# First q stacks computed in place, four first products moved into block 0, v's bias sent through the projection

## The chip, the core and the metric

The kernel runs on one NeuronCore of a Trainium2 chip. The metric is the device time of one execution in microseconds (us); a time is the median of several runs. The engines are TensorE (PE; PEld is its weight load), VectorE (DVE), ScalarE (ACT), GpSimd (POOL) and SyncE (SP, which only issues DMAs). Each works through its own instruction list in order and waits on semaphores. TensorE writes to PSUM; ACT and DVE read PSUM and write SBUF.

## What is computed

Layer 0 is attention over the 4096 pixels of each of 4 images with 128 channels, layer 1 two quantized 3x3 convolutions with batch norm. Only layer 0 bears on the change:

```python
x_norm = group_norm(x, norm_w, norm_b)                  # 8 groups
qkv = einsum('oc,bchw->bohw', qkv_w, x_norm) + qkv_b
q, k, v = split(qkv)                                    # 4 heads of 32 channels
attn = softmax(einsum('bhid,bhjd->bhij', q, k) * d**-0.5)
out = einsum('bhij,bhjd->bhid', attn, v)
out = einsum('oc,bchw->bohw', proj_w, out) + proj_b
x = x + out
```

Each row of the softmax sums to one, so a constant added to v comes out of the attention unchanged, and the projection of that constant can be added to proj_b.

## The kernel before

The kernel tries `_fast_body` and has a general version behind it that isn't run with these inputs. Everything named here is in `_fast_body`, which writes the order of all instructions by hand.

**Tiling.** The 4096 pixels of an image are NB = 8 chunks of 512 (FB) for k, v and q, and NK = 32 key tiles of 128. A block is one image and one chunk of 512 queries: 32 blocks. For each key tile of a block, `scores` (L442) makes two score halves of 128 keys by 2 heads by 512 queries with 4 matmuls each, and ACT turns each into exponentials p (L444). `weights` (L456) multiplies v by p in two halves of 4 matmuls each and adds into acc. Most p tiles are added into r by DVE (L469, L471); those of the key tiles in MOVED are added into rm by DMAs from POOL (L464, L466). At a block's end, `finish_parts` copies acc, merges rm into r, takes the sums l, inverts, weighs, projects (po), adds the bias bp and the residual (L547) and stores y0.

**Groups.** The main loop is `run_scores(3); run_weights(3)`: a group is three score halves, then three weight halves. TensorE runs three score halves ahead. `schedule` attaches side work to weight halves of a block: `at_half(p, f)` calls f after half p. `ends[i]` is the last half of the block's group i. `visit(i, first, second, evacuate, split=False)` puts both halves of a product after `ends[i]` and its emptying one half later. That is in the next group, so on ACT it stands behind the three exponentials of that group.

**Products.** A k, q or v product is one chunk through the normed weights `wn`: `banded` (L317) makes it with one matmul for each head into a band of 32 partitions. k and q are split into a high and a low part in fp32r: ACT writes the high part with the bias (L351), DVE the low part (L352). Both parts are staged, written to DRAM (kd, qd; L356) and loaded back as stacks, in which each head has its high and its low part on two bands of 32 partitions (`load_k` L411, `load_q` L422). v is emptied by DVE alone, which adds v's bias (L371).

**Buffers.** [...]The pool `pss` has three tiles of two banks, named "s", for scores; the pool `psa` has two tiles of one bank, named "a". In a block acc holds one of these two; everything else that TensorE writes outside scores (products, sums, projection, the small matmuls of the norm) goes through the other. During the start-up k and q products use `pss`. In a block the parts of k are staged in one buffer named "k", those of q1 in one named "q"; in the start-up they use tiles of the pool of p.

**Start-up.** Eight chunks of image 0 are loaded into two tiles. DVE takes their statistics (L597). `norm_parts` works out the norm in small steps: `four` makes wn and a vector c (scaled mean less bias), `five` and `six` the biases of k and q from c (L281, L282, L286), `five_v` and `six_v` v's bias as a 128 by 128 tile, the same on all partitions (L291, L296). Then the list

```python
for what, j in (("k", 0), ("q", 0), ("k", 1), ("v", 0), ("k", 2), ("v", 1), ("k", 3), ("v", 2),
                ("k", 4), ("v", 3)):
```

is worked off, and the scores begin. The stacks of k0 and q0 don't go through DRAM: `direct` copies them by eight DMAs each from the staged parts (L402 for k from SP and POOL, L404 for q from ACT, SP and POOL). The other eight first products (k5, v4, k6, v5, k7, q1, v6, v7) are attached to block 0, after the ends 0, 2, 4 and so on to 14 in steps of two groups. q2 to q7 of image 0 are made in block 1.

**Later images.** The norm of image b + 1 is prepared during image b. In the fourth block of image 0 (third of images 1 and 2), `five` is called after `ends[1]`, `six` and `five_v` one half later, `six_v` two halves later, and the first k product of the next image follows after `ends[3]`.

Of the kernel before, what the change touches and what calls it, by code (L numbers as in the profile page):

```python
# [16 lines left out]
F32 = mybir.dt.float32  # L17
AF = mybir.ActivationFunctionType
ALU = mybir.AluOpType
# [3 lines left out]
P = 128  # L23
GROUP = 16
HEADS = 4
D = 32
TAPS = 9
FB = 512
# [50 lines left out]
def _fast_body(ctx, tc, x, norm_w, norm_b, qkv_wt, qkv_b, proj_wt, proj_b,  # L79
               w1, alpha1, gamma1, beta1, w2, alpha2, gamma2, beta2, out, cnt):  # L80
    nc = tc.nc
# [6 lines left out]
    KB = FB // P  # L88
# [26 lines left out]
    nw, nb = column(norm_w, "nw"), column(norm_b, "nb")  # L115
    wqkv = const.tile([P, 3 * P], F32, name="wqkv")
    nc.gpsimd.dma_start(out=wqkv, in_=qkv_wt)
    bkq = const.tile([P, 2], F32, name="bkq")
    nc.gpsimd.dma_start(out=bkq[:, 0:1], in_=qkv_b[P : 2 * P].rearrange("(c o) -> c o", o=1))
    nc.gpsimd.dma_start(out=bkq[:, 1:2], in_=qkv_b[0:P].rearrange("(c o) -> c o", o=1))  # L120
    bv = const.tile([P, P], F32, name="bv")
    nc.gpsimd.dma_start(out=bv, in_=qkv_b[2 * P : 3 * P].partition_broadcast(P))
    wp = const.tile([P, P], F32, name="wp")
    nc.gpsimd.dma_start(out=wp, in_=proj_wt)
    bp = column(proj_b, "bp")
# [101 lines left out]
    def f32(t):  # L227
        return t.bitcast(F32)
# [8 lines left out]

    norm = {}  # L240

    def norm_parts(b, st):
        mv = small.tile([P, 2], F32, name=f"mv{b}", tag="mv")
        mean = small.tile([P, 1], F32, name=f"mean{b}", tag="mean")
        dv = small.tile([P, 1], F32, name=f"dv{b}", tag="dv")
        gm = {}

        def zero():
            nc.vector.bn_aggr(mv, st.rearrange("p j s -> p (j s)"))


        def one():
# [12 lines left out]
        def four():  # L265
            r = rsqrt_eps(gm[1][:, 0:1], f"gr{b}")
            a = small.tile([P, 1], F32, name=f"ga{b}", tag="ga")
            nc.vector.tensor_tensor(a, r, nw, ALU.mult)
            c = small.tile([P, 1], F32, name=f"gc{b}", tag="gc")
            nc.vector.scalar_tensor_tensor(c, mean, a, nb, ALU.mult, ALU.subtract)  # L270
            wn = wpool.tile([P, 3 * P], F32, name=f"wn{b}", tag="wn")
            nc.vector.tensor_scalar(wn, wqkv, a, None, ALU.mult)
            cb = wpool.tile([P, P], F32, name=f"cb{b}", tag="cb")
            nc.vector.tensor_copy(cb, c.to_broadcast([P, P]))
            norm[b] = [wn, c, cb]


        def five():
            wn, c, cb = norm[b]
            gm[2] = psa.tile([P, FB], F32, name=f"gb{b}", tag="a")  # L280
            nc.tensor.matmul(gm[2][:, 0:1], wqkv[:, P : 2 * P], c, start=True, stop=True)  # L281
            nc.tensor.matmul(gm[2][:, 1:2], wqkv[:, 0:P], c, start=True, stop=True)  # L282

        def six():
            b2 = wpool.tile([P, 2], F32, name=f"b2_{b}", tag="b2")
            nc.vector.tensor_tensor(b2, bkq, gm[2][:, 0:2], ALU.subtract)  # L286
            norm[b][1] = b2

        def five_v():
            gm[3] = psa.tile([P, FB], F32, name=f"gw{b}", tag="a")  # L290
            nc.tensor.matmul(gm[3][:, 0:P], norm[b][2], wqkv[:, 2 * P : 3 * P],  # L291
                             start=True, stop=True)

        def six_v():
            bvn = wpool.tile([P, P], F32, name=f"bvn{b}", tag="bvn")
            nc.vector.tensor_tensor(bvn, bv, gm[3][:, 0:P], ALU.subtract)  # L296
            norm[b][2] = bvn

        return zero, one, two, three, four, five, six, five_v, six_v

# [18 lines left out]
    def project_parts(b, j, xin, start=False):  # L319
# [3 lines left out]
        ps = {}  # L323
# [23 lines left out]
        def parts(what, o, dst):  # L347
            t = staged(2, what)
            bias = norm[b][1][:, o : o + 1]
            hi, lo = (t[:, i, :].bitcast(F32R) for i in range(2))  # L350
            nc.scalar.activation(hi, ps[what], AF.Identity, bias=bias)  # L351
            nc.vector.scalar_tensor_tensor(lo, ps[what], bias, t[:, 0, :], ALU.add, ALU.subtract)  # L352
            if start and j == 0:
                direct(what, t)
            else:
                (nc.sync if start else nc.gpsimd).dma_start(out=dst[b, j].rearrange("s p n -> p s n"), in_=t)  # L356

# [7 lines left out]
        def evac_v():  # L365
            if b == 0:
                v = vs[b, j] = vpool.tile([P, KB, P], F32, name=f"v{b}_{j}", tag="v")
                v = v.rearrange("p i f -> p (i f)")
            else:
                v = staged(1, "v")[:, 0, :]  # L370
            nc.vector.tensor_tensor(v.rearrange("p (i f) -> p i f", f=P),  # L371
                                    ps["v"].rearrange("p (i f) -> p i f", f=P),
                                    norm[b][2].unsqueeze(1).to_broadcast([P, KB, P]), ALU.add)
            if b > 0:
                nc.gpsimd.dma_start(out=vd[b, j], in_=v)

# [6 lines left out]
    def k_tile(b, j):  # L383
        ks[b, j] = stack_tile(f"k{b}_{j}")[:, : 2 * FB].rearrange("p (g n) -> p g n", n=FB)
        return ks[b, j]

    def q_tile(b, j):
        qs[b, j] = qpool.tile([P, 2, 2, FB], F32R, name=f"q{b}_{j}", tag="q")
        return qs[b, j]

    def direct(what, t):

        u = k_tile(0, 0) if what == "k" else q_tile(0, 0)
        engines = (nc.sync, nc.gpsimd) if what == "k" else (nc.scalar, nc.sync, nc.gpsimd)
        for g in range(2):
            for c, s in enumerate((0, 2, 1, 3)):
                i, part = divmod(s, 2)
                h = 2 * g + i
                src = t[h * D : (h + 1) * D, :, :]
                eng = engines[(4 * g + c) % len(engines)]  # L400
                if what == "k":
                    eng.dma_start(out=f32(u)[s * D : (s + 1) * D, g, :], in_=src[:, part, :])  # L402
                else:
                    eng.dma_start(out=f32(u)[s * D : (s + 1) * D, g, :, :], in_=src)  # L404

    def load_k(b, j):
        k = k_tile(b, j)
        for s in range(4):
            i, part = divmod(s, 2)
            src = kd[b, j][part].rearrange("(g i d) n -> i d g n", i=2, d=D)  # L410
            nc.sync.dma_start(out=f32(k)[s * D : (s + 1) * D, :, :], in_=src[i])  # L411
# [61 lines left out]
    def finish_parts(n):  # L473
# [70 lines left out]
            banded(t["o"], wp, av)  # L544

        def store():
            nc.vector.scalar_tensor_tensor(t["x"], t["o"], bp, t["x"], ALU.add, ALU.add)  # L547
            nc.gpsimd.dma_start(out=y0[b][:, qb * FB : (qb + 1) * FB], in_=t["x"])

        return dict(copy=copy, merge=merge, sums=sums, sums_at_once=sums_at_once, bounds=bounds,  # L550
# [44 lines left out]
    st = small.tile([P, NB, 6], F32, name="st0", tag="st")  # L595
    for j in range(NB):
        nc.vector.bn_stats(st[:, j, :], halves[j // 4][:, j % 4, :])  # L597
    zero, one, two, three, four, five, six, five_v, six_v = norm_parts(0, st)
    zero()
    one()  # L600
    keep_warm(3)
# [11 lines left out]
        load_k(b, j)  # L613
        load_v(b, j)

    for what, j in (("k", 0), ("q", 0), ("k", 1), ("v", 0), ("k", 2), ("v", 1), ("k", 3), ("v", 2),
                    ("k", 4), ("v", 3)):
        for f in first_chunk(j, what, True):
            f()
        if what == "q":  # L620
            five_v()
            six_v()
        if what == "v":
            load_k(0, j + 1)

# [7 lines left out]
    def schedule(n, before):  # L633
# [5 lines left out]
        def at_half(p, f):  # L639
            todo.append((p, f))  # L640
# [25 lines left out]
        if n + 1 < len(blocks):  # L666
            add(22 if n == 0 else 14, lambda: load_q(*blocks[n + 1]))
        if n == 0:
            for i, what, j in ((0, "k", 5), (2, "v", 4), (4, "k", 6), (6, "v", 5), (8, "k", 7),
                               (10, "q", 1), (12, "v", 6), (14, "v", 7)):  # L670
                visit(i, *first_chunk(j, what, False), split=False)
                if what == "k":
                    at_half(ends[i] + 5, lambda j=j: load_k(0, j))
# [9 lines left out]
        if b + 1 < B:  # L683
# [10 lines left out]
            if qn == 2:  # L694
                at_half(ends[1], late[b][5])
                at_half(ends[1] + 1, late[b][6])
                at_half(ends[1] + 1, late[b][7])
                at_half(ends[1] + 2, late[b][8])
            if b == 0:
                chunks = {2: (), 3: (0, 1), 4: (2, 3), 5: (4, 5), 6: (6,), 7: (7,)}  # L700
            else:
                chunks = {1: (), 2: (0, 1), 3: (2, 3), 4: (4,), 5: (5,), 6: (6,), 7: (7,)}
# [708 lines left out]
```

## Time and profile before

| | |
|---|---|
| time, median of 3 runs | 2549.02 us (2548.26 to 2549.62) |
| the profiled execution | 2548.74 us, span 2547.0 us |
| granted TensorE clock, mean | 0.995 |
| first scores start | 26.66 us |
| weights of block 0 start | 31.91 us |
| TensorE busy in 34.2 to 92.0 us | 57.80 of 57.80 us |
| the same for ACT, DVE | 50.10, 49.16 us |
| low part (L352) of a k or q chunk | 0.75 us |
| high part (L351) | 0.69 us |
| v with its bias (L371) | 0.68 us |
| one addition to r (L471) | 2.29 us |

The profile is that of one execution; its times start with the span. Timeline rows give start and duration in us, the engine, the line, the operation, output and inputs with their shapes, and a count where neighbouring instructions of one kind are merged. Brackets hold how long the engine stood idle ahead of the row and what released it. In the chain of work that ended last, a piece lasts until the next begins. An fp32 matmul appears as two passes, so a count of 16 is 8 matmuls; the fp32r matmuls of the scores appear as one.

### The profile page before, as it was taken

The page shows a single profiled execution, that of the slowest core. Times are in us where ns is not written, and L with a number is a line of the kernel's source. Part 1 is how long each engine was busy: PE and PEld are TensorE (multiplying, and loading weights), DVE is VectorE, ACT ScalarE, POOL GpSimd, SP SyncE. Part 2 cuts the span into 40 slices and gives each one's busy share as a digit, 9 for nine tenths or more (in the row PEclk, how much of TensorE's full clock was granted, in tenths as well). Part 3 has the DMA queues.
Part 4 walks back from the last instruction along what each step waited for, and adds up shares of the span by engine and source line. Part 5 has one row for each costly group of instructions (what it writes and reads, how often), then busy time and mean ns, then how long its engine had stood idle before and what let it go on. Part 6 is the DMA issues. An engine that isn't in the chain of part 4 may idle for free.

```text
span 2547.0 us, 65043 instructions
## 1 busy us (share of the span) xinstructions
PE 2509.0 (99%) x28708; PEld 1503.6 (59%) x28708; DVE 2137.2 (84%) x1402; ACT 2087.4 (82%) x2278; POOL 281.6 (11%) x461
## 2 busy tenths in 40 slices
PE   9999999999999999999999999999999999999995
PEld 6555555555555555555555555555555555577774
DVE  6899888889988889889988888889999999954445
ACT  5999888999988999999988899989999999911224
POOL 2111111111011111110111111111000011000000
PEclk9999999999999999999999999999999999999998
DMA  6877667788757667797766666796666666745004
GB/s 193 192 185 169 168 173 181 171 203 182 184 132 190 170 152 169 164 231 164 173 163 172 157 166 158 191 203 150 149 138 144 146 145 149 150 90 160 1 1 166
DMA packets 148954, 403.86 MB, mean 159 GB/s; under 512 B 59416, under 2 KB 60184, under 8 KB 120120
## 3 DMA queue, kind: packets, MB, share of 16 engines
q0 software_dynamic: 45840, 280.39, 48.2%
q1 hardware_dynamic: 100952, 113.60, 16.9%
q10 hardware_dynamic: 1872, 5.64, 0.6%
q8 instruction: 227, 3.72, 0.6%
q14 instruction: 63, 0.52, 0.1%
HBM read 107.48 MB, written 56.42 MB: 64 GB/s over the span
## 4 chain that ended last, share of the span: by engine, by line
PE 92%; issue 3%; DMA 2%; DVE 1%; ACT 1%; ACTq 0%; POOL 0%; SPq 0%; POOLq 0%; DVEq 0%
PE s L442 41%; PE acc L456 36%; PE c L782 9%; DMA rm<-p 2%; PE l L488 1%; PE pq L317 1%; PE pk L317 1%; PE po L317 1%; PE pv L317 1%; DVE r L471 1%; ACT p L444 0%; ACT res L949 0%; DMA xh<-in_x_dram 0%; PE c_last L782 0%; DVE res L948 0%
## 5 line engine op out<-in xcount | busy, mean ns | idle before, releaser
L444 ACT ACTIVATE p<-s 128x1024 f32<-128x1024 f32 x2048 | 1950.5, 1032 | 201.6 <-PE s L442 154.5
L471 DVE TENSOR_TENSOR r<-r,p 128x2048 f32<-128x2048 f32 x768 | 1758.2, 2289 | 65.0 <-ACT p L444 14.5
L442 PE MATMUL s<-q,k 64*128 64x512 f32 x8192 | 1138.6, 409 | 1.7 <-ACT p L444 0.9
L456 PE MATMUL acc<-p,v 128*32 128x256 f32 x16384 | 1026.4, 383 | 0.0
L442 PEld LDWEIGHTS s<-q,k 64*128 64x128 f32 x8192 | 715.4, 184 | 410.3 <-issue 165.3
L456 PEld LDWEIGHTS acc<-p,v 128*32 128x32 f32 x16384 | 462.4, 109 | 483.7 <-issue 248.5
L466 POOL DMA_DIRECT2D rm<-p x160 | 139.5, 872 | 800.4 <-ACT p L444 535.5
L849 ACT COPY cv<-c 128x512 f32<-128x512 f32 x60 | 35.2, 586 | 200.1 <-DVE st L848 200.1
L782 PE MATMUL c<-hi,wq 128*128 128x512 f32 x540 | 139.1, 401 | 1.3 <-issue 1.3
L782 PE MATMUL c<-lo,wq 128*128 128x512 f32 x540 | 138.5, 400 | 0.0
L848 DVE BATCH_NORM_STATS2 st<-c 128x6 f32<-128x512 f32 x60 | 41.9, 699 | 103.9 <-PE c L782 83.4
L782 PEld LDWEIGHTS c<-hi,wq 128*128 128x128 f32 x540 | 101.2, 188 | 30.3 <-issue 2.1
L782 PEld LDWEIGHTS c<-lo,wq 128*128 128x128 f32 x540 | 101.6, 188 | 27.2
L352 DVE SCALAR_TENSOR_TENSOR kst<-pk,b,kst 128x512 fp32r<-128x512 f32 x32 | 24.0, 751 | 83.6 <-PE s L442 68.5
L469 DVE TENSOR_TENSOR r<-p,p 128x2048 f32<-128x2048 f32 x32 | 73.2, 2288 | 12.1 <-ACT p L444 11.1
L352 DVE SCALAR_TENSOR_TENSOR qst<-pq,b,qst 128x512 fp32r<-128x512 f32 x32 | 24.0, 751 | 58.2 <-PE s L442 47.3
L356 POOL DMA_DIRECT2D qd<-qst x31 | 23.6, 760 | 262.7 <-DVE qst L352 220.8
L492 POOL DMA_DIRECT2D r<-rm x31 | 26.2, 844 | 220.4 <-DMA rm<-p 95.1
L356 POOL DMA_DIRECT2D kd<-kst x27 | 20.0, 740 | 175.8 <-DVE kst L352 167.2
L488 PE MATMUL l<-r,ones 128*32 128x256 f32 (+1 forms) x504 | 37.7, 382 | 0.0
L464 POOL DMA_DIRECT2D rm<-p x32 | 17.8, 557 | 176.8 <-ACT p L444 93.4
L351 ACT ACTIVATE kst<-pk,b 128x512 fp32r<-128x512 f32 x32 | 22.3, 699 | 18.2 <-PE pk L317 18.2
(149 smaller groups left out, 739.3 us busy)
## 6 DMA issues: line engine op xcount, KB each, us to landing
rm<-p POOLq DMA_DIRECT2D x192, 1024.0 KB, 7.9
q<-qd SPq DMA_DIRECT2D x248, 128.0 KB
r<-rm POOLq DMA_DIRECT2D x31, 1024.0 KB, 7.6
x<-in_x_dram SPq DMA_DIRECT2D x86, 256.0 KB
k<-kd SPq DMA_DIRECT2D x124, 128.0 KB
qd<-qst POOLq DMA_DIRECT2D x31, 512.0 KB, 5.3
kd<-kst POOLq DMA_DIRECT2D x27, 512.0 KB, 4.8
y<-x POOLq DMA_DIRECT2D x32, 256.0 KB, 6.2
```

The lines of the kernel that those rows point to most:

```text
L317: nc.tensor.matmul(out[cs, :], w[:, cs], x, start=True, stop=True)
L352: nc.vector.scalar_tensor_tensor(lo, ps[what], bias, t[:, 0, :], ALU.add, ALU.subtract)
L356: (nc.sync if start else nc.gpsimd).dma_start(out=dst[b, j].rearrange("s p n -> p s n"), in_=t)
L442: nc.tensor.matmul(s[:, i, :], k[r, half, c0 : c0 + P], q[r, half, part, :], start=(part == 0), stop=(part == 1))
L444: nc.scalar.activation(pts[step][:, 2 * half : 2 * half + 2, :], s, AF.Exp, scale=SCALE)
L456: nc.tensor.matmul(acc[n][h * D : (h + 1) * D, cs], v[:, kt % KB, h * D : (h + 1) * D], pt[:, h, cs], start=(kt == 0 and half == 0), stop= ...
L466: nc.gpsimd.dma_start(out=msum[n], in_=pt, accum_op=ALU.add)
L469: nc.vector.tensor_tensor(rsum[n], pts[step - 1], pt, ALU.add)
L471: nc.vector.tensor_tensor(rsum[n], rsum[n], pt, ALU.add)
L488: nc.tensor.matmul(t["l"][h * D : (h + 1) * D, cs], ones, r[:, h, cs], start=first, stop=end)
L782: nc.tensor.matmul(ps.rearrange("p (r w) -> p r w", w=W), w[:, tap, :], part[:, r0 + kh : r0 + kh + RB, kw : kw + W], start=(n == 0), stop ...
L848: nc.vector.bn_stats(st[:, b * NB + c, :], ps[:, j, :])
```

## The change

- q0 is computed straight into its stack (`direct_q`). For each pair of heads g, four matmuls of 512 columns with the 32 weight columns of a head go into four bands, so that each head's product stands on two bands. ACT writes the high part and DVE the low part of all 128 partitions into the q tile, with biases that are laid out in the same way: four more small DMAs load them into columns 2 and 3 of bkq, and `five` makes eight more one-column matmuls for image 0. Nothing is staged, and `direct` is left with k0.
- The start-up list loses k3, v2, k4 and v3; they are attached to block 0, in which twelve products now follow the ends 0, 1, 2, 4, 5, 6, 8, 9, 10, 11, 13 and 14.
- v is copied without its bias. The bias is a column u; `seven_v` multiplies it by the projection's weights and `eight_v` adds the result to bp. The output takes this column in place of bp. In the start-up both are called behind the list; for later images `seven_v` is attached to `ends[3]`, `eight_v` to the half after it.

```diff
-    bkq = const.tile([P, 2], F32, name="bkq")
+    bkq = const.tile([P, 4], F32, name="bkq")
...
-    bv = const.tile([P, P], F32, name="bv")
-    nc.gpsimd.dma_start(out=bv, in_=qkv_b[2 * P : 3 * P].partition_broadcast(P))
+    for band in range(4):
+        nc.gpsimd.dma_start(
+            out=bkq[band * D : (band + 1) * D, 2:4],
+            in_=qkv_b[0:P].rearrange("(g i d) -> i d g", i=2, d=D)[band // 2])
+    bv = const.tile([P, 1], F32, name="bv")
+    nc.gpsimd.dma_start(out=bv, in_=qkv_b[2 * P : 3 * P].rearrange("(c o) -> c o", o=1))
...
-            cb = wpool.tile([P, P], F32, name=f"cb{b}", tag="cb")
-            nc.vector.tensor_copy(cb, c.to_broadcast([P, P]))
...
+            if b == 0:
+                for g in range(2):
+                    for band in range(4):
+                        h = 2 * g + band // 2
+                        nc.tensor.matmul(gm[2][band * D : (band + 1) * D, 2 + g : 3 + g],
+                                         wqkv[:, h * D : (h + 1) * D], c, start=True, stop=True)
...
-            nc.tensor.matmul(gm[3][:, 0:P], norm[b][2], wqkv[:, 2 * P : 3 * P],
-                             start=True, stop=True)
+            nc.tensor.matmul(gm[3][:, 0:1], wqkv[:, 2 * P : 3 * P], gc[b], start=True, stop=True)
...
+            u = small.tile([P, 1], F32, name=f"bvn{b}", tag="bvn")
+            nc.vector.tensor_tensor(u, bv, gm[3][:, 0:1], ALU.subtract)
+            gm[4] = u
+
+        def seven_v():
+            gm[5] = psa.tile([P, FB], F32, name=f"gp{b}", tag="a")
+            nc.tensor.matmul(gm[5][:, 0:1], wp, gm[4], start=True, stop=True)
+
+        def eight_v():
+            norm[b][2] = small.tile([P, 1], F32, name=f"bpn{b}", tag="bpn")
+            nc.vector.tensor_tensor(norm[b][2], bp, gm[5][:, 0:1], ALU.add)
...
-            nc.vector.tensor_tensor(v.rearrange("p (i f) -> p i f", f=P),
-                                    ps["v"].rearrange("p (i f) -> p i f", f=P),
-                                    norm[b][2].unsqueeze(1).to_broadcast([P, KB, P]), ALU.add)
+            nc.vector.tensor_copy(v, ps["v"])
...
+    def direct_q(xin):
+
+        u = q_tile(0, 0)
+        ps = pss.tile([P, 2, FB], F32, name="pq_first", tag="s")
         for g in range(2):
+            for band in range(4):
+                h = 2 * g + band // 2
+                nc.tensor.matmul(ps[band * D : (band + 1) * D, g, :], norm[0][0][:, h * D : (h + 1) * D],
+                                 xin, start=True, stop=True)
+            bias = norm[0][1][:, 2 + g : 3 + g]
+            nc.scalar.activation(u[:, g, 0, :], ps[:, g, :], AF.Identity, bias=bias)
+            nc.vector.scalar_tensor_tensor(u[:, g, 1, :], ps[:, g, :], bias, f32(u)[:, g, 0, :],
+                                           ALU.add, ALU.subtract)
...
-            nc.vector.scalar_tensor_tensor(t["x"], t["o"], bp, t["x"], ALU.add, ALU.add)
+            nc.vector.scalar_tensor_tensor(t["x"], t["o"], norm[b][2], t["x"], ALU.add, ALU.add)
...
-    for what, j in (("k", 0), ("q", 0), ("k", 1), ("v", 0), ("k", 2), ("v", 1), ("k", 3), ("v", 2),
-                    ("k", 4), ("v", 3)):
+    for what, j in (("k", 0), ("q", 0), ("k", 1), ("v", 0), ("k", 2), ("v", 1)):
+        if what == "q":
+            direct_q(halves[0][:, 0, :])
+            five_v()
+            six_v()
+            continue
...
+    seven_v()
+    eight_v()
...
-            for i, what, j in ((0, "k", 5), (2, "v", 4), (4, "k", 6), (6, "v", 5), (8, "k", 7),
-                               (10, "q", 1), (12, "v", 6), (14, "v", 7)):
+            for i, what, j in ((0, "k", 3), (1, "k", 4), (2, "v", 2), (4, "k", 5), (5, "v", 3),
+                               (6, "v", 4), (8, "k", 6), (9, "v", 5), (10, "q", 1), (11, "k", 7),
+                               (13, "v", 6), (14, "v", 7)):
...
+                at_half(ends[3], late[b][9])
+                at_half(ends[3] + 1, late[b][10])
```

More of the change, by code (lines that the diff above doesn't have):

```diff
@@ L236, in load_x @@
         return t
-    norm = {}
+    norm, gc = {}, {}
     def norm_parts(b, st):
@@ L272, in four @@
             nc.vector.tensor_scalar(wn, wqkv, a, None, ALU.mult)
-            cb = wpool.tile([P, P], F32, name=f"cb{b}", tag="cb")
-            nc.vector.tensor_copy(cb, c.to_broadcast([P, P]))
-            norm[b] = [wn, c, cb]
+            norm[b] = [wn, c, None]
+            gc[b] = c
         def five():
-            wn, c, cb = norm[b]
+            wn, c, _ = norm[b]
             gm[2] = psa.tile([P, FB], F32, name=f"gb{b}", tag="a")
@@ L282, in five @@
             nc.tensor.matmul(gm[2][:, 1:2], wqkv[:, 0:P], c, start=True, stop=True)
+            if b == 0:
[4 more added lines that the diff above has]
+                                         wqkv[:, h * D : (h + 1) * D], c, start=True, stop=True)
         def six():
-            b2 = wpool.tile([P, 2], F32, name=f"b2_{b}", tag="b2")
-            nc.vector.tensor_tensor(b2, bkq, gm[2][:, 0:2], ALU.subtract)
+            n = 2 if b else 4
+            b2 = wpool.tile([P, 4], F32, name=f"b2_{b}", tag="b2")
+            nc.vector.tensor_tensor(b2[:, :n], bkq[:, :n], gm[2][:, :n], ALU.subtract)
             norm[b][1] = b2
@@ L290, in five_v @@
             gm[3] = psa.tile([P, FB], F32, name=f"gw{b}", tag="a")
-            nc.tensor.matmul(gm[3][:, 0:P], norm[b][2], wqkv[:, 2 * P : 3 * P],
-                             start=True, stop=True)
+            nc.tensor.matmul(gm[3][:, 0:1], wqkv[:, 2 * P : 3 * P], gc[b], start=True, stop=True)
         def six_v():
[L295 to L299, printed above, removed]
+            u = small.tile([P, 1], F32, name=f"bvn{b}", tag="bvn")
[7 more added lines that the diff above has]
+            nc.vector.tensor_tensor(norm[b][2], bp, gm[5][:, 0:1], ALU.add)
+        return zero, one, two, three, four, five, six, five_v, six_v, seven_v, eight_v
     kd, qd, vd = {}, {}, {}
@@ L353, in parts @@
             if start and j == 0:
-                direct(what, t)
+                direct_k(t)
             else:
@@ L389, in q_tile, with direct_k @@
         return qs[b, j]
-    def direct(what, t):
-        u = k_tile(0, 0) if what == "k" else q_tile(0, 0)
-        engines = (nc.sync, nc.gpsimd) if what == "k" else (nc.scalar, nc.sync, nc.gpsimd)
-        for g in range(2):
[L396 to L404, printed above, removed]
+    def direct_k(t):
+        u = k_tile(0, 0)
+        for c, (g, s) in enumerate((g, s) for g in range(2) for s in (0, 2, 1, 3)):
+            i, part = divmod(s, 2)
+            h = 2 * g + i
+            (nc.sync, nc.gpsimd)[c % 2].dma_start(out=f32(u)[s * D : (s + 1) * D, g, :],
+                                                  in_=t[h * D : (h + 1) * D, part, :])
+    def direct_q(xin):
+        u = q_tile(0, 0)
+        ps = pss.tile([P, 2, FB], F32, name="pq_first", tag="s")
+        for g in range(2):
+            for band in range(4):
[6 more added lines that the diff above has]
+                                           ALU.add, ALU.subtract)
     def load_k(b, j):
@@ L597, in _fast_body @@
         nc.vector.bn_stats(st[:, j, :], halves[j // 4][:, j % 4, :])
-    zero, one, two, three, four, five, six, five_v, six_v = norm_parts(0, st)
+    zero, one, two, three, four, five, six, five_v, six_v, seven_v, eight_v = norm_parts(0, st)
     zero()
@@ L614, in load_kv @@
         load_v(b, j)
-    for what, j in (("k", 0), ("q", 0), ("k", 1), ("v", 0), ("k", 2), ("v", 1), ("k", 3), ("v", 2),
-                    ("k", 4), ("v", 3)):
+    for what, j in (("k", 0), ("q", 0), ("k", 1), ("v", 0), ("k", 2), ("v", 1)):
[4 more added lines that the diff above has]
+            continue
         for f in first_chunk(j, what, True):
             f()
-        if what == "q":
-            five_v()
-            six_v()
         if what == "v":
             load_k(0, j + 1)
+    seven_v()
+    eight_v()
     late, xin = {}, {}
```

## Prediction

> **What bounds the kernel now.** I read the page's shares and chain first, then the start-up, the first block of attention and the set-up of a batch in the timeline, and last the order and the semaphore waits of the changed program as built (no time is in those).
>
> ```profile
> PE 2509.0 (99%) x28708; PEld 1503.6 (59%) x28708; DVE 2137.2 (84%) x1402; ACT 2087.4 (82%) x2278; POOL 281.6 (11%) x461
> ...
> PE 92%; issue 3%; DMA 2%; DVE 1%; ACT 1%; ACTq 0%; POOL 0%; SPq 0%; POOLq 0%; DVEq 0%
> ```
>
> TensorE is busy for 99% of the span and is 92% of the chain that ended last; a matmul added, or a wait put in front of one, goes to the end in full. The start-up on TensorE:
>
> ```profile
> 22.00 1.05 PE L317 MATMUL pk<-xh,wn 128*32 128x256 f32 x16
> 23.91 1.08 PE L317 MATMUL pv<-wn,xh 128*32 128x128 f32 x32 [0.87 <-DVE v L371]
> ...
> 26.66 0.74 PE L442 MATMUL s<-q,k 64*128 64x512 f32 x4
> 28.09 2.06 PE L442 MATMUL s<-q,k 64*128 64x512 f32 x12 [0.69 <-DVE v L371]
> ...
> 31.91 1.50 PE L456 MATMUL acc<-p,v 128*32 128x256 f32 x24
> ```
>
> [...]The first scores follow the last product (26.66), and the weights of the first block begin at 31.91. From there TensorE has no gap. A product in the block, and who empties its bank:
>
> ```profile
> 33.23 1.05 PE L317 MATMUL pk<-xh,wn 128*32 128x256 f32 x16
> 34.21 1.67 PE L442 MATMUL s<-q,k 64*128 64x512 f32 x12
> 34.98 2.85 ACT L444 ACTIVATE p<-s 128x1024 f32<-128x1024 f32 x3 [1.04 <-PE s L442]
> 35.80 1.50 PE L456 MATMUL acc<-p,v 128*32 128x256 f32 x24
> 37.24 1.67 PE L442 MATMUL s<-q,k 64*128 64x512 f32 x12
> 37.71 0.70 ACT L351 ACTIVATE kst<-pk,b 128x512 fp32r<-128x512 f32 x1
> 38.44 0.75 DVE L352 SCALAR_TENSOR_TENSOR kst<-pk,b,kst 128x512 fp32r<-128x512 f32 x1 [4.01 <-PE s L442]
> 39.49 0.73 POOL L356 DMA_DIRECT2D kd<-kst  x1 [16.80 <-DVE kst L352]
> 40.16 1.06 PE L317 MATMUL pv<-wn,xh 128*32 128x128 f32 x32
> ```
>
> A group of three score halves and three weight halves takes 37.24 - 34.21 = 3.03 us. The product of the group before is emptied only after the group's three exponentials, because its instructions stand behind them on ACT: DVE ends at 38.44 + 0.75 = 39.19, which is 4.98 after the group began. It costs nothing here, since the next product comes two groups later (40.16).
>
> [...]The changed q product has its halves in two banks of one tile, yet the built program makes the second half wait for DVE's reading of the first.[...]
>
> **The change, part by part.** All sums are against the profiled execution's 2548.74 us (span 2547.0, 1.74 around it); the median of the runs is 0.28 above.
>
> *Start-up.* The eight extra bias matmuls for q's bands stand before the first product. One matmul is two passes in the trace (x2), so 16 passes. Bounds: [...]at most 16 times the 110 ns mean of a 32-column load, 1.76. The 16 loads of the same shape in pk span 0.59; I take 0.8. The first k product starts at 17.0 instead of 16.22, and its ACT part at 18.15 (1.14 later, as before). q's first half is four 512-column matmuls, as po, whose path is 0.86; it ends near 18.75. The second half waits for DVE: k's high part 18.15 to 18.85, q's on ACT 18.95 to 19.7; on DVE k's low part to 19.62, then q's to 20.45. TensorE stands 1.75 and starts the half at 20.5. Then 0.86 for it, 0.3 for the v bias, and k1, v0, k2, v1 at 0.86 each: 25.1. The projected bias waits for v0's copy, which DVE reaches after q's second low part (23.05), the bias and k1's low part (24.25): about 24.9, so no stand; 0.3 for it. Scores start at 25.4. k0's own DMAs (issues from 18.9, four on SP at 0.58, landing 2.2 as on POOL) are there at 23.7. Three exponentials from 26.15 at 1.02 let the sixth score go at 29.25; weights start at 29.9: **gain 2.0**. The eight q-stack DMAs that ACT, SP and POOL issue go away; ACT's three (19.72 to 21.73) stood ahead of k1's high part, and the clock above has them out. The four added bias loads push POOL's later loads back by 4 x 0.53 us; the last issue then ends at about 14.4, just ahead of the power for the norm (14.62): nothing, or up to 0.5 if a load's semaphore is late.
>
> *Four products moved into block 0*: 4 x 0.86 (the chain's piece for one) = **+3.5**, all on TensorE.
>
> *Their spacing.* The block's products now stand at group ends 0, 1, 2, 4, 5, 6, 8, 9, 10, 11, 13, 14 and no longer at every second one. The built program shows k4's first matmul waiting for k3's low part, and v2's for k4's. After a k or q product the bank is free 4.98 + 0.04 into the next group, where the next product would start at 3.03: 2.0 of standing. That happens for k3 to k4, k4 to v2, k5 to v3, k6 to v5 and q1 to k7: **+10.0**. Behind the waiting matmul stand the next group's scores, so ACT runs dry and gives nothing back. A v product is emptied by DVE alone, about 3.2 after its group begins, or at once where DVE was waiting for it: v3 to v4 and v5 to q1 nothing, v6 to v7 **+0.4** (0 to 0.8).
>
> *Staging buffer.* k3 and k4 now use the one staged buffer for k. ACT's high part of k4 must wait for k3's write: issue at 6.27 after product k3 began (39.49 - 33.23), landing 4.8 to 5.3 later, so 11.1 to 11.5; ACT would be there at 6.0 + 0.98 + 3.5 = 10.5. **+0.8** (0 to 1.2).
>
> *Set-up of batches 1 to 3.* The projected v bias is a matmul at the same half as a k product, so k waits for DVE's add of it, and the add stands behind a sum of r:
>
> ```profile
> 739.67 1.50 PE L456 MATMUL acc<-p,v 128*32 128x256 f32 x24
> 739.91 2.29 DVE L471 TENSOR_TENSOR r<-r,p 128x2048 f32<-128x2048 f32 x1 [0.24 <-ACT p L444]
> 740.99 1.05 PE L317 MATMUL pk<-x,wn 128*32 128x256 f32 x16
> ```
>
> Here DVE is busy to 742.20, the add ends near 742.4, and k could have started at 741.1: 1.3. In the other two blocks DVE is free 0.6 us before; there matmul, signal and add are 0.5 each. Together 2.3, less 0.1 three times, as the v bias is a one-column matmul (0.32 on the path) in place of a 128-column one (0.42): **+2.0** (0.5 to 3).
>
> *At nothing*: v's copy for the add (0 to 0.1 each, DVE not last), the output's other bias column, the copy of c that is dropped (0.22 on DVE beside TensorE).
>
> Sum: -2.0 + 3.5 + 10.0 + 0.8 + 0.4 + 2.0 = +14.7, so 2563.4 beside 2548.74 and **2563.7 us** beside the median.
>
> **Rivals.** *The waits are void* (not slower): when TensorE reaches each added wait, it is already met. It decides where k's low part is done within 3.03 us of the group's start, and not at 4.98. Then the 11.2 and the 2.3 go, and 1.75 in the start-up: -2.0 - 1.75 + 3.5 - 0.3 = -0.55, 2548.5 us. Against it: ACT's order is fixed in the built program, and each k and q in block 0 shows about 4.98. 4%. *Only the spacing is free* (some wait of the "a" buffers is met): -2.0 + 3.5 + 2.0 = +3.5, 2552.5 us. Against it the same; for it only that ACT and DVE have slack. 8%. *Stacks come late as well*: k1's load was complete near 33.3 (last issue ended 31.28, 2 for landing), and the changed kernel wants it near 33.2; k7's chain took 16.3 us from its product, 60.92, to its stack, some 77.2, against 19.1 between product and use. For it: the writes stand in POOL's queue beside the 1 MB sums. Against: q's 1 MB of direct copies and two writes leave the start-up. If both slip, some +4: 2567.7 us. 12%. The forecast has 76%.
>
> **How the numbers follow.** The forecast's own terms reach from about 2559 to 2568 (bias matmuls -0.4 to +1.0, each stand 1.7 to 2.1, staging, v and set-up as bounded, start-up gain 0.5 to 3.5). With the late stacks above and part of the way to the free spacing below, the range is 2556 to 2570; it leaves out the two cheap rivals (12%) and tails of 8%. 0.2%, 5.1 us, is about what a measurement of this kernel can tell from no change: slower 87% (forecast and late stacks, less 1), the same 11% (both cheap rivals fall here, at -0.5 and +3.5), faster 2%.
>
> **What would show it.** In the profile after: TensorE idle of 1.5 to 2 us before pq_first's second half; weights of block 0 near 30; idle near 2 us before k4, v2, v3, v5 and k7 with DVE's low part as releaser, a little more before v2; 0.5, 1.3 and 0.5 before the first k product of each later batch. I am wrong if those products show no idle time, if ACT's low or high parts come ahead of the exponentials, or if block 0 ends as early as before.

## The result, and the profile after

| | before | after |
|---|---|---|
| median (6 runs each, on one chip) | 2548.81 us (2546.05 to 2550.02) | 2566.19 us (2562.88 to 2568.8) |
| ratio to before, 95% interval | | 1.0069 [1.0056, 1.0082] |
| profiled execution | 2548.74 us, span 2547.0 | 2568.8 us, span 2566.8 |

The changed kernel is 17.4 us slower. 2563.7 was predicted, range 2556 to 2570. The profiled execution after is the slowest of its six runs, so its own sum (19.8 us of span) is larger than that of the medians.

The page's shares and the chain by engine, after:

```profile
PE 2515.8 (98%) x28732; PEld 1505.5 (59%) x28732; DVE 2137.3 (83%) x1403; ACT 2088.5 (81%) x2279; POOL 284.2 (11%) x465
...
PE 88%; DMA 4%; issue 3%; DVE 2%; ACT 1%; POOL 0%; SPq 0%; ACTq 0%; POOLq 0%; DVEq 0%
```

TensorE's share of the chain falls from 92% to 88%, and its busy time rises by 6.8 us, though the change adds only a few one-column matmuls. So the loss has two forms: TensorE stands, and TensorE works more slowly. The line numbers of the changed kernel are others: products L336, scores L467, exponentials L469, weights L481, the high part of k and q L370 and its low part L371. The start-up on TensorE, after:

```profile
15.18 0.31 PE L292 MATMUL gb<-gc,wqkv 128*32 128x1 f32 x16
15.33 1.05 PE L336 MATMUL pk<-xh,wn 128*32 128x256 f32 x16
16.19 1.04 PE L424 MATMUL pq_first<-xh,wn 128*32 128x512 f32 x8
18.83 1.06 PE L424 MATMUL pq_first<-xh,wn 128*32 128x512 f32 x8 [1.59 <-DVE q L428]
19.82 0.38 PE L303 MATMUL gw<-gc,wqkv 128*128 128x1 f32 x2
20.14 1.92 PE L336 MATMUL pk<-xh,wn 128*32 128x256 f32 x16
21.82 1.94 PE L336 MATMUL pv<-wn,xh 128*32 128x128 f32 x32
23.53 1.09 PE L336 MATMUL pk<-xh,wn 128*32 128x256 f32 x16
...
30.09 1.50 PE L481 MATMUL acc<-p,v 128*32 128x256 f32 x24
```

The stand ahead of q's second half is there (1.59). The two products after it take 1.92 and 1.94 where each of the others takes 1.05. The windows of that stretch say why (the third number from the end is the granted TensorE clock):

```profile
20.10:21.80 1.70, 1.70 (x17) 0.83 (x21) 0.81 (x2) 0.55 (x1) 0.67 (x2) 0.53 0.66 138
21.80:23.50 1.70, 1.70 (x36) 1.63 (x32) 0.67 (x1) 0.69 (x1) 0.00 (x0) 0.50 0.02 0
23.50:25.40 1.90, 1.90 (x56) 1.37 (x47) 0.78 (x2) 0.69 (x1) 0.00 (x0) 0.97 0.48 175
```

The granted clock reads 0.50 from 20.20 to 23.62. Block 0 on TensorE, after:

```profile
37.43 1.07 PE L336 MATMUL pk<-xh,wn 128*32 128x256 f32 x16 [1.94 <-DVE kst L371]
38.43 1.66 PE L467 MATMUL s<-q,k 64*128 64x512 f32 x12
40.02 1.50 PE L481 MATMUL acc<-p,v 128*32 128x256 f32 x24
43.55 1.47 PE L336 MATMUL pv<-wn,xh 128*32 128x128 f32 x32 [2.03 <-DVE kst L371]
44.95 2.82 PE L467 MATMUL s<-q,k 64*128 64x512 f32 x12
47.70 1.50 PE L481 MATMUL acc<-p,v 128*32 128x256 f32 x24
```

k4 stands 1.94 for the low part of k3, v2 stands 2.03 for that of k4, and three scores after it take 2.82 in place of 1.66: the clock again, 0.50 from 44.10 to 47.51. TensorE's list of waits, after (total, times, longest):

```profile
PE pv L336 <- DVE kst L371: 6.0, 3, 2.0
...
PE pk L336 <- DVE qst L371: 1.9, 1, 1.9
PE pk L336 <- DVE kst L371: 1.9, 1, 1.9
...
PE pq_first L424 <- DVE q L428: 1.6, 1, 1.6
PE pk L336 <- DVE bpn L316: 1.3, 3, 0.8
```

None of these five is in the list of before. The first three lines are the five adjacent products, the last is the set-ups of three images. The longest of its waits, 0.8, is in block 10; the timeline of all engines after, there:

```profile
757.49 2.29 DVE L496 TENSOR_TENSOR r<-r,p 128x2048 f32<-128x2048 f32 x1 [0.35 <-ACT p L469]
...
758.70 0.38 PE L312 MATMUL gp<-bvn,wp 128*128 128x1 f32 x2
...
759.70 0.15 DVE L316 TENSOR_TENSOR bpn<-bp,gp 128x1 f32<-128x1 f32 x1
```

DVE's sum ends at 759.78 by its row; the add for the bias comes directly behind it, and the k product only after that, at 759.90: the case that the prediction read from the row of 2.29 at 739.91.

**Where the time went in the profiled execution.** Three marks split it: the first bias matmul of the norm (gb), the first weights, and the copy of acc at a block's end. x reached the chip earlier in this execution (DVE's last statistics of it start at 9.91, 11.18 before), and gb came 1.04 earlier (14.64, 15.68 before). This is chance: gb starts at 14.81 in e5 and e8, at 15.28 in e4 and at 17.42 in e3.

| stretch | before | after | difference |
|---|---|---|---|
| gb to first weights | 16.23 | 15.45 | -0.78 |
| first weights to the end of block 0 | 72.52 | 89.56 | +17.04 |
| three set-ups (blocks 3, 10, 18) | | | 0.65 + 1.36 + 0.67 = +2.68 |
| start of gb | 15.68 | 14.64 | -1.04 |
| the rest to the last block's end | | | +2.12 |

The sum is 20.02. The rest stands in blocks 7 to 9, 14 to 16, 23 and 24, of both signs: waits of the projection po for DVE (block 7 +1.34, block 23 -1.49), one of the norm's small matmul for DVE (1.10 in block 9) and one of the scores for ACT, which itself waited for a DMA of p (1.34 in block 16). For the first of these no step of the change is seen: e11 below has 2.4 more in block 7 by such a wait, e8 none. Block 16 is open: nine of the ten kernels with the projected bias take 0.9 to 1.6 more there than the kernel before, e8 and e7 (which keeps v's bias) take 0.01 more. In block 10, 0.11 of the 1.36 is another wait, that of gw for a bias (0.77 after, 0.66 before).

Block 0's 17.04 divides by its rows: four products 3.5; five stands 1.94 + 2.03 + 1.96 + 2.00 + 1.94 = 9.87; about 0.2 after each, since a group with a stand takes 6.04 where one with a product takes 3.90; the slow clock after v2 1.58 (v2 0.4, scores 1.16); v6 to v7 0.35; late stacks 0.84 (below).

### The profile page after: what moved, and what is told of

It reads as the page before. It is cut to its first block, busy times and chain, and to the rows that moved or that the text cites. A ratio compares the mean times of both kernels' runs of the same rounds, so it can differ in the third digit from the quotient of the medians.

```text
span 2566.8 us, 65081 instructions
## 1 busy us (share of the span) xinstructions
PE 2515.8 (98%) x28732; PEld 1505.5 (59%) x28732; DVE 2137.3 (83%) x1403; ACT 2088.5 (81%) x2279; POOL 284.2 (11%) x465
## 4 chain that ended last, share of the span: by engine, by line
PE 88%; DMA 4%; issue 3%; DVE 2%; ACT 1%; POOL 0%; SPq 0%; ACTq 0%; POOLq 0%; DVEq 0%
PE s L467 39%; PE acc L481 35%; PE c L813 9%; DVE r L496 2%; DMA rm<-p 2%; DMA rc<-rd 1%; PE pk L336 1%; PE l L513 1%; PE pv L336 1%; PE po L336 1%; PE pq L336 1%; ACT p L469 1%; DMA q<-qd 1%; ACT res L980 0%; PE c_last L813 0%
## 5 line engine op out<-in xcount | busy, mean ns | idle before, releaser
L469 ACT ACTIVATE p<-s 128x1024 f32<-128x1024 f32 x2048 | 1950.3, 1031 | 221.2 <-PE s L467 175.3
L467 PE MATMUL s<-q,k 64*128 64x512 f32 x8192 | 1139.7, 409 | 2.7 <-ACT p L469 2.7
L481 PE MATMUL acc<-p,v 128*32 128x256 f32 x16384 | 1026.4, 383 | 0.0
L467 PEld LDWEIGHTS s<-q,k 64*128 64x128 f32 x8192 | 716.1, 185 | 411.0 <-issue 169.1
L481 PEld LDWEIGHTS acc<-p,v 128*32 128x32 f32 x16384 | 462.4, 109 | 483.6 <-issue 248.4
L371 DVE SCALAR_TENSOR_TENSOR kst<-pk,b,kst 128x512 fp32r<-128x512 f32 x32 | 24.0, 751 | 94.8 <-PE s L467 63.8
L371 DVE SCALAR_TENSOR_TENSOR qst<-pq,b,qst 128x512 fp32r<-128x512 f32 x31 | 23.3, 751 | 60.2 <-PE s L467 46.6
L573 POOL DMA_DIRECT2D y<-x x32 | 22.4, 700 | 131.4 <-DVE x L572 121.3
```

The lines of the kernel that those rows point to most:

```text
L467: nc.tensor.matmul(s[:, i, :], k[r, half, c0 : c0 + P], q[r, half, part, :], start=(part == 0), stop=(part == 1))
L469: nc.scalar.activation(pts[step][:, 2 * half : 2 * half + 2, :], s, AF.Exp, scale=SCALE)
L481: nc.tensor.matmul(acc[n][h * D : (h + 1) * D, cs], v[:, kt % KB, h * D : (h + 1) * D], pt[:, h, cs], start=(kt == 0 and half == 0), stop= ...
```

## The experiments

Each ratio is to the kernel before on the same chip. The kernel before had a median of 2548.35 us beside the first four, 2547.3 beside the second four, 2547.8 beside the last two. The two stretches that decide are the same as above (gb to weights; weights to the end of block 0).

| kernel | time, us | ratio to before | gb to weights | block 0 |
|---|---|---|---|---|
| before | | 1 | 16.23 | 72.52 |
| after | 2566.19 | 1.0069 [1.0056, 1.0082] | 15.45 | 89.56 |
| e1: emptied in the own group | 2553.01 | 1.0019 [1.001, 1.0027] | 13.77 | 80.63 |
| e2: four products back | 2551.31 | 1.0011 [1.0003, 1.002] | 17.24 | 72.44 |
| e3: q in two tiles | 2563.55 | 1.0057 [1.0044, 1.0071] | 13.98 | 91.43 |
| e4: matmuls in the stand | 2565.83 | 1.0076 [1.0062, 1.009] | 13.77 | 89.25 |
| e5: projected bias earlier | 2564.74 | 1.0068 [1.0055, 1.0082] | 13.76 | 89.33 |
| e7: moved products alone | 2563.05 | 1.0061 [1.0047, 1.0074] | 16.47 | 89.07 |
| e8: e1 with a second buffer | 2549.95 | 1.0013 [1.0006, 1.0019] | 13.77 | 76.02 |
| e9: e8, e3 and e5 together | 2547.33 | 1.0002 [0.9994, 1.0011] | 11.96 | 76.04 |
| e10: e2, e3 and e5 together | 2546.9 | 0.9999 [0.9991, 1.0007] | 15.44 | 72.43 |
| e11: e9, v1 between scores | 2547.52 | 1.0001 [0.9992, 1.0009] | 11.38 | 76.06 |

**e1: block 0's products emptied in their own group.**

```diff
-                at_half(e + 1, evacuate)
+                at_half(e if n == 0 else e + 1, evacuate)
```

> The changed kernel, but in block 0 each product is emptied at once, ahead of the next group's exponentials and not behind them. If the cost lies in the spacing (TensorE standing 1.9 to 2.0 us before k4, v2, v3, v5, k7, some 0.2 more to fill up again, and a halved clock after the first two), all five stands go and with them the slow stretch at 45: 5 x 2.15 + 1.6 = 12 us less, some 2554. If the cost lies in the four products themselves and in stacks that come late, only late stacks can improve: at most 1 us less, 2565.

All five stands are gone, and so are the late stacks; 13 of the 17 us with them. One new stand has come. The timeline of all engines of e1:

```profile
38.82 0.69 ACT L370 ACTIVATE kst<-pk,b 128x512 fp32r<-128x512 f32 x1 [4.26 <-DMA kd<-kst]
39.41 2.84 ACT L469 ACTIVATE p<-s 128x1024 f32<-128x1024 f32 x3
...
40.48 0.41 PE L481 MATMUL acc<-p,v 128*32 128x256 f32 x2 [2.57 <-ACT p L469]
...
40.73 1.61 PE L336 MATMUL pv<-wn,xh 128*32 128x128 f32 x28
```

ACT holds k4's high part back for 4.26 us until k3's write has left the one staging buffer; the exponentials queue behind it on ACT, and TensorE waits 2.57 for them. This is the step that the prediction priced at 0.8. In the changed kernel it isn't seen, because there k4 is itself 2 us late. Here too the clock falls after the stand, to 0.50 from 42.30 to 44.00: the next scores take 2.84 (1.67 in e9), v2 some 0.6 more.

**e2: the four products back in the start-up**, with the old ends in block 0. q in place and the projected bias stay.

```diff
-    for what, j in (("k", 0), ("q", 0), ("k", 1), ("v", 0), ("k", 2), ("v", 1)):
+    for what, j in (("k", 0), ("q", 0), ("k", 1), ("v", 0), ("k", 2), ("v", 1), ("k", 3), ("v", 2),
+                    ("k", 4), ("v", 3)):
...
```

> The changed kernel with the four products back in the start-up and the old eight ends in block 0; q's stack in place and v's bias through the projection stay. If the moved products carry the loss (17 us in block 0 against 3.5 for the products in the start-up), some 13 us less: 2552 to 2554, the rest being the stand before q's second half, the slow clock behind it and the three set-ups. If the q and bias parts carry it, 2560 or more.

Block 0 takes 72.44, as before. What is left against the kernel before is the start-up's 17.24 - 16.23 = +1.01 and the set-ups: block 3 +0.68, block 10 +0.91, block 18 +0.68. So q in place, with its stand of 1.59, doesn't pay by itself. The four products are worth 17.24 - 13.77 (e1, the same start-up without them) = 3.47 there, where 3.5 was predicted.

**e3: q's halves in two PSUM tiles; e4: six matmuls of the filler kind in the stand.**

```diff
-        ps = pss.tile([P, 2, FB], F32, name="pq_first", tag="s")
         for g in range(2):
+            ps = pss.tile([P, 2, FB], F32, name=f"pq_first{g}", tag="s")
...
```

```diff
         for g in range(2):
+            if g == 1:
+                keep_warm(6)
```

> The changed kernel with q's two halves in two PSUM tiles, so that the second half waits for nobody. The stand of 1.6 us goes; if the halved clock from 20.1 to 23.5 is a consequence of this stand, 1.6 more: 3.2 us less, 2563. If the clock falls for another reason, only 1.6 less and k1 and v0 still take twice their time.

> The changed kernel with six idle matmuls of 128 columns on TensorE between q's two halves, in the time in which it stands; nothing is waited for less. If standing lowers the clock, k1 and v0 take 0.87 each and not 1.7, so 1.6 us less, 2564.6. If the wait and not the idleness is the cost, the same time as the changed kernel or more, with the clock still at 0.5.

Two tiles take the stand away: q's halves are one row of 16 passes (1.90 us in e9, with the same edit). In e3's profiled execution the norm came late instead (its first matmul waited 2.96 for its statistics), and the matmuls behind that wait were slow: twelve filler passes took 2.77 (1.60 in e8), and ACT reached k0's high part 1.98 after the product began (1.12 in e5). The 13.98 holds about 2.0 of this (e9 has 11.96 with the same start-up). e4 keeps TensorE busy in the stand, and k1 and v0 take no longer than in e5 (in both, ACT reaches k1's part 1.31 after q's second, k2's 1.74 later; 2.15 and 2.58 after); its time of 2565.83 is no better than the changed kernel's. As a cure of the clock e4 is inconclusive, and the next kernels show why: e5 and e8 have the stand of 1.59 without the filler, and are not slowed behind it (the clock of e8 reads 1.00 from 14 to 30, and e5 takes 13.76 where e8 takes 13.77). The start-up of e8:

```profile
16.36 1.04 PE L426 MATMUL pq_first<-xh,wn 128*32 128x512 f32 x8
19.00 1.06 PE L426 MATMUL pq_first<-xh,wn 128*32 128x512 f32 x8 [1.59 <-DVE q L430]
19.99 0.38 PE L303 MATMUL gw<-gc,wqkv 128*128 128x1 f32 x2
20.30 1.07 PE L336 MATMUL pk<-xh,wn 128*32 128x256 f32 x16
21.19 1.06 PE L336 MATMUL pv<-wn,xh 128*32 128x128 f32 x32
```

The same stand, and k1 takes 1.07 here, 1.92 after.

**e5: the projected bias of images 1 to 3 attached one group earlier.**

```diff
-                at_half(ends[3], late[b][9])
-                at_half(ends[3] + 1, late[b][10])
+                at_half(ends[2], late[b][9])
+                at_half(ends[2] + 1, late[b][10])
```

> The changed kernel with the projected v bias of images 1 to 3 attached one group earlier, so that DVE has added it before the first k product. If the three added waits are what sets 2.7 us of the loss, the waits of pk for bpn are gone from TensorE's list, the marks of blocks 3, 10 and 18 no longer lose 0.65, 1.36 and 0.67, and the time falls from 2566.2 to about 2563.5 (ratio to the kernel before 1.006). If the stands only cover another limit (a late DVE, a late load), a wait of the same size stands elsewhere in those blocks and the time stays at 2566.

The waits for bpn are gone, and the three marks now give +0.38, -0.26 and +0.21 in place of 0.65, 1.36 and 0.67: 2.35 less. Of this 0.59 isn't the edit's: ahead of it in block 10 gw waits 0.18 for a bias here, 0.77 after. So 1.76 is saved in the profile. TensorE of e5 in block 10:

```profile
754.88 0.38 PE L312 MATMUL gp<-bvn,wp 128*128 128x1 f32 x2
755.20 1.67 PE L467 MATMUL s<-q,k 64*128 64x512 f32 x12
756.80 1.50 PE L481 MATMUL acc<-p,v 128*32 128x256 f32 x24
758.12 1.05 PE L336 MATMUL pk<-x,wn 128*32 128x256 f32 x16
```

A group lies between the bias matmul and k. The time can't show this: the ratios are 1.0068 here and 1.0069 after, and the interval is 2.7 thousandths, 7 us, wide. The profile decides this one.

**e7: the kernel before with only the two lists of the change** (six products in the start-up, twelve in block 0).

> The kernel before with only the start-up list and the twelve ends of block 0 of the change: q0 still goes through its direct copies, v keeps its bias. If the closer products cost what the stands show, the five stands (10.9 with their refill), v6 to v7 (0.4) and the late stacks (0.8) come back whole, the moved products are neutral (3.5 less in the start-up, 3.5 more in the block), and the time is 2560 to 2564, 12 to 16 above the kernel before. If the stands come from the in-place q or from v's copy on DVE, it stays near the kernel before, 2549 to 2552. If q0's copies have not landed when the shorter list ends, the scores wait for them, and 1 to 2 us of the 3.5 is lost in the start-up.

2563.05 us: nearly the whole loss comes from this part, and block 0's 89.07 is that of the full change. The gain of the shorter list is not there: 16.47 to the first weights, 16.23 before. TensorE of e7:

```profile
20.64 1.06 PE L317 MATMUL pv<-wn,xh 128*32 128x128 f32 x32
24.84 0.76 PE L442 MATMUL s<-q,k 64*128 64x512 f32 x1 [3.14 <-DMA q<-qst]
26.07 5.67 PE L442 MATMUL s<-q,k 64*128 64x512 f32 x23 [0.47 <-DMA q<-qst]
31.67 1.50 PE L456 MATMUL acc<-p,v 128*32 128x256 f32 x24
```

With fewer products ahead of them the scores wait 3.6 us for q's direct copies, and behind the wait they are slow: 23 matmuls take 5.67, about 0.25 each, where twelve take 1.67 in block 0, 0.14 each. The expectation had 1 to 2 us for this. An estimate: in e8 the weights come 4.34 after the first scores; counted from 26.07, this would leave a gain of 1.2 without the slow matmuls. So of the 3.5 about 2.3 went to the wait and the rest to the slow matmuls, and the parts of the change belong together: with q's stack coming by DMA, the shorter list gained nothing here.

**e8: e1, and k4's parts in the staging buffer that q1 uses later.**

```diff
                 tag = "kq"[j % 2] if what == "q" and b == 0 else what
+                if b == 0 and what == "k" and j == 4:
+                    tag = "q"
```

> The run that empties block 0's products within their own group, and with it k4's parts in the staging buffer that q1 uses later. If the single staging buffer makes the 2.6 us stand at 40.5 of that run and the stand the slow clock after it (1.2), both are gone, and the time falls from 2553.0 to 2549 to 2550: the start-up gain, 0.8 to 2, then pays for 2.7 of the set-ups in part. If ACT was late there because its emptying stands between exponentials, and not because of k3's write, the stand remains and the time stays at 2553.

The stand of 2.57 and the slow clock behind it are gone (the clock reads 1.00 from 30 to 106). Block 0 takes 76.02, which is 72.52 and the four products (3.50), with nothing else. The marks leave 4.6 between e1 and e8; the ratios, 1.0019 and 1.0013, agree in sign, but with intervals that overlap.

**e9: all repairs together** (the edits of e8, e3 and e5). **e10: e2 with the edits of e3 and e5**, that is the change without moving anything. **e11: e9, and v1's product between the third and the fourth score half:**

```diff
...
     run_scores(3)
+    for f in first_chunk(1, "v", True):
+        f()
```

> All repairs together: emptying within the own group, k4's second staging buffer, q's halves in two tiles, the projected bias one group earlier. By the sum of the parts: no stands in block 0 (3.5 for the products, paid by the shorter list), none in the set-ups, 1.6 less in the start-up: 2545 to 2547, 2 to 3 below the kernel before. If the stands hid other limits (late stacks of k1 or k7, the ready time of weights), these come out and the time is 2549 or above.

> The change without the four moved products (old start-up list, old ends in block 0), with q's halves in two tiles and the projected bias one group earlier. If moving products is neutral on TensorE (3.5 out of the start-up, 3.5 into the block) and only its waits cost, this equals the repaired full change, 2546 to 2548 where the kernel before has 2547.3; weights start near 30.8 and block 0 ends 1 before the kernel before. If the shorter list is worth something of its own, this is 1 to 3 slower than the repaired change.

> The repaired full change with v1's product put between the third and the fourth score half, where TensorE waits for ACT three times 0.18 and 0.4 in sum otherwise. If TensorE's own work sets the start of the weights, nothing is won (weights at 27.3, 2547). If the first exponentials set it, the product is hidden and the weights start up to 0.9 earlier: 2546 to 2546.5. A loss of 0.5 or more would mean that v1's copy on DVE or its bank delays the first weights.

The start-up of e9:

```profile
16.01 1.05 PE L336 MATMUL pk<-xh,wn 128*32 128x256 f32 x16
16.87 1.90 PE L426 MATMUL pq_first<-xh,wn 128*32 128x512 f32 x16
18.70 0.38 PE L303 MATMUL gw<-gc,wqkv 128*128 128x1 f32 x2
19.02 1.07 PE L336 MATMUL pk<-xh,wn 128*32 128x256 f32 x16
```

e9's start-up is 4.27 shorter than before and its block 0 3.52 longer, so the repaired change nets -0.75, and +0.26 in the set-ups (0.7 without a shorter wait of gw in block 10, 0.21 for 0.66). That is below what can be measured: 1.0002. The 2 to 3 us below the kernel before that were expected are not there. e10 moves nothing and nets 15.44 - 16.23 = -0.79: the same. e11 hides v1's 0.87 in part (11.38 for 11.96), and its time doesn't show it. None of the three beats the kernel before by more than the measurement's uncertainty.

## Why the prediction was right, point by point

**The mechanism held.** The products in adjacent groups wait for the part of DVE that empties the one free bank; e1 takes the lateness away and the stands go, e7 has the stands without the rest of the change. The terms, as measured in the profiled execution:

| term | predicted | measured |
|---|---|---|
| start-up, gb to weights | -2.0 | -2.46 at full clock; -0.78 with the slow clock |
| four products | +3.5 | +3.5 (e8: 76.02 - 72.52) |
| five stands | 5 x 2.0 = +10.0 | 9.87, and some 0.2 behind each: +10.9 |
| v6 to v7 | +0.4 | +0.35 |
| staging buffer | +0.8 | 0; 2.57 in e1 |
| set-ups | +2.0 | +2.7 |
| slow clock in block 0 | not foreseen | +1.58 |
| late stacks | rival, 4 | +0.84 |

Against the 14.7 of the prediction the measured terms come to some 19 in this one execution, and 3.3 of the difference is the slow clock (1.68 and 1.58), which the sum left out. The medians are 17.4 apart. That 2563.7 lies only 2.5 from the median is in part luck: the staging buffer and the start-up were priced too high by 0.8 and 0.5, against the clock, the refill behind the stands and the late stacks.

*Start-up.* The step that failed is the price of the eight bias matmuls. They put the first product off by 0.15 (15.18 to 15.33; from gb to that product 0.69, before 0.54), where 0.8 was taken; the range went down to 0.4, which was the author's estimate and which no trace of before shows. The trace after has about 10 ns a pass. This makes the gain larger, 2.46 in e8 and 2.47 in e5. The stand was 1.59 for 1.75, but that gained nothing: q's second half starts 3.50 after the first product, as in the working (20.5 - 17.0). In the profiled execution after, 1.68 of that went to the clock. The weights at 30.09 beside the predicted 29.9 look exact and are not: gb came 1.04 early, and the clock cost 1.68.

*Clock.* The prediction took matmuls at one duration throughout. In the profiled execution after, the granted clock has two levels while TensorE works: it reads 0.50 from 20.20 to 23.62, behind the stand of 1.59, and from 44.10 to 47.51, behind that of 2.03, and 1.00 in the rest of 6.55 to 2542. In e1 it reads 0.50 from 42.30 to 44.00, behind the stand of 2.57; in e5 from 56 to 58, with TensorE idle for 1.95 between 52 and 55. For e3, e4 and e7 ACT's waits for the first scores behind a stand of block 0 tell the same. They are 2.61 and 2.62 behind k4 and v3 after, where the clock reads 1.00, and 3.50 and 3.51 where it reads 0.50 (behind v2 after, behind v3 in e5). Behind v2 they are 3.12 in e3, 2.62 in e4 and 2.63 in e7, behind v3 3.87, 3.66 and 3.63. So in block 0 every profiled execution with these stands had at least one slow stretch, behind v2 (after, e3) or v3 (e3, e4, e5, e7). Behind the single stand of the start-up only one of five had one (after; the clock of e1, e2 and e8 reads 1.00 from 14 to 30, and e5's start-up is as long as e8's). What separates two equal stands was not shown: these are single executions, and no run moved a stand against another or changed its length alone.

*Staging.* Both times of the working were right: ACT reached k4's high part 10.62 after product k3 began (42.03 - 31.41; 10.5 predicted), and k3's write was issued at 6.26 (6.27). The failed part is the landing. It was taken as 4.8 to 5.3, where the writes of k's parts in block 0 of the kernel before show 4.9, 4.8 and also 4.1; k3's landed 4.3 us after its issue, at 41.97, just ahead of ACT. So there was no wait here, because k4 was late by its own stand. Where the stand is taken away (e1), k4 comes 2 us earlier, k3's write lets go 5.98 after its issue, and the wait is dearer than priced, 2.57 on TensorE, as the exponentials stand behind it.

*Set-ups.* Predicted 0.5, 1.3 and 0.5 less 0.3; measured 0.65, 1.36 and 0.67. e5 shows that most of this is the wait for the add: without it +0.81 is left, the wait of gw in block 10 set aside (+0.33 with it). With that wait aside block 10 is 1.25, and all three were a little dearer than predicted; none went the way of the low bound.

*At nothing.* v's copy takes 0.68 us after (L390), as the add with the bias did before (L371, 0.68).

*Rivals.* "The waits are void" and "only the spacing is free" fall with the five stands. "Stacks come late as well" is true in a small part: not k1, but the first scores that need k7, and the first of block 1, which need q1. TensorE after, with the row of an undisturbed three scores first:

```profile
100.11 1.66 PE L467 MATMUL s<-q,k 64*128 64x512 f32 x12
...
103.13 2.03 PE L467 MATMUL s<-q,k 64*128 64x512 f32 x12
...
112.59 2.14 PE L467 MATMUL s<-q,k 64*128 64x512 f32 x12
```

0.37 and 0.47. In the second the weight loads wait for q's DMA; for the first the trace names no releaser, and k7 is taken from its place (the ninth weight load of the twelve is the first on k7's keys, and the gap follows it). e8, in which the products are emptied and written earlier, has neither.

*Moved products.* That they are neutral by themselves (3.5 out, 3.5 in) is shown by e9 and e10. What the prediction didn't ask is whether the shorter start-up list could be used at all: e7 shows that with the old copies it gained nothing.

## What to carry to other kernels

Before a producer is put into every group in place of every second, take the time from its start to the release of its buffer (4.98 us here) and compare it with the period (3.03): the difference is paid once for each neighbour, and the engine that all the work goes through pays it in full. The cure was to empty the buffer earlier on ACT and to give the staged data a second buffer, one place each in the code; removing only the first wait uncovered the second. Work that was moved from one stretch of the bound engine to another stretch of it gained nothing here (e9 and e10): look for a place in which that engine stands.

## What the runs showed that was not expected

- Stands of TensorE of 1.59 to 2.57 us were followed by a stretch of slow clock in some executions and not in others. In the profiled execution after, the clock read 0.50 for 3.4 us in the start-up and again in block 0, which cost 1.68 and 1.58. The six kernels in which block 0 has stands of about 2 us or more (after, e1, e3, e4, e5, e7) all show slow matmuls behind one there; the six without (before, e2, e8, e9, e10, e11) show a clock of 1.00 in every stretch from 14 to 106 us.
- Sixteen passes of one column over four bands took 0.15 us, about 10 ns each.
- In this program a PSUM tile of two banks is waited for as a whole: the matmuls into its second bank stood 1.59 us for the reading of the first. In two tiles of the pool they didn't: the sixteen passes are one row of 1.90 us (e9, e10, e11).
